# A graph-attention layer: in the steps of the softmax chain, look products ahead of kept-back products

## The chip, the cores and the metric

The kernel runs on one core of one Trainium2 chip. Its engines are TensorE (PE in the profile, with its weight loads as PEld), VectorE (DVE), ScalarE (ACT), GpSimd (POOL) and SyncE (SP). The metric is the device time of one execution in microseconds, median of three runs.

## The reference

12500 nodes with 64 features, 400000 edges with 64 features. Edges are sorted by destination, sources are random. Cut to what matters:

```
h_src = x[src]; h_dst = x[dst]
e     = leaky_relu(concat(h_src, h_dst, ef) @ W_attn + b_attn, 0.01)
m     = concat(h_src, ef) @ W_ne
emax  = segment_max(e, dst);  ex = exp(e - emax[dst])
alpha = ex / segment_sum(ex, dst)[dst]
z     = segment_sum(alpha * m, dst)
out   = relu(concat(x, z) @ W_out)
result = layernorm(x + out)
```

## The kernel before, in words

The edges are cut into groups of 512 (128 partitions times T = 4). Destinations are uneven: many edges go to the first nodes. Most groups go through 41 chunks of up to 16 groups, and a chunk through 4 lots of 4 groups. A chunk's course:

- **Gather.** For each group and t, POOL issues one indirect DMA (L331) that fetches 128 rows of a table by the edges' sources: 64 rows per chunk, numbered 0 to 63. POOL works a chunk ahead. The function `gather` ties certain rows to the step markers of the chunk in front (L53, below): row 28 is held until the last TensorE instruction that step 0 of the softmax had, row 33 until step 1's, 42 and 48 until step 2's and step 3's, 56 and 61 until the chunk's first and second products.
- **Scores.** VectorE and ScalarE work out the edge scores of each lot (L371 to L392).
- **Softmax.** A chain over the whole chunk (`softmax`, from L695 to L757): VectorE scans, two small matmuls to turn a column into a line (L599), a scan of the tops on one partition (L707, L708), a copy on ScalarE (L606, `line`), two small matmuls back into a column (L602), VectorE again from L717, L722 and L737 on ScalarE, and the same passage by L599, L741/L742, L606 and L602 for the denominators, then from L750 to L757 the weights. The chain has four breaks, in which TensorE would otherwise wait: `drawn` runs `dense_step(n)` there for n = 0 to 3.
- **Products.** `some_products` multiplies weighted one-hot destinations with gathered rows (L804, L809), two groups at a time, into a PSUM bank; VectorE adds the banks up (L828). Of a chunk's four lots two are multiplied right after the softmax; the other two are kept back ("later") and done in the softmax steps of the next chunk: four groups in step 0, two each in steps 1 and 2.

A second class of groups, 128 "dense" ones, is worked off beside the chunks. For each there is a *look* and a *count*. A look needs a one-hot row: `look_row` (L421) loads a row of 128 KB into the one buffer `low_of`, `look_turn` (L431, L432, ScalarE) makes the one-hot tile `big` from it, `look_products` (L442) makes four matmuls with it, each with a weight load and each shown as two instructions, into a bank of the ring `pg` (4 banks), and `look_scores` (L469 to L475, VectorE) picks the scores from them. A count (`dense_counts`) makes four tiles on ScalarE (L483, L484) and lows on VectorE (L486) and multiplies them (L491). Chunks 0 to 31 have looks: 128 in all, five in most of the first 18 chunks with looks, three or four in the others. The first of a chunk is made ahead of the softmax, the others in its steps: 96 of them, in 32 chunks.

The order of each engine is written by hand: what is called first in the program stands first in each engine's queue. So the order of calls in `dense_work(n)` is the order in which TensorE, ScalarE, VectorE and SP see that step's work. `seen` holds looks whose products were made, `turns` the one-hot tiles, `rows_ahead` the loaded rows. `latest()` returns the last TensorE instruction issued so far; behind each step it becomes the step's marker.

```
BEHIND = ((28, 0), (33, 1), (42, 2), (48, 3), (56, "first"), (61, "second"))
```

Of the kernel before, what the change touches and what calls it, by code (L numbers as in the profile page):

```python
# [59 lines left out]
def sorted_path(ctx, tc, x, dst, idx, edge, w_ne, w_attn, b_attn, w_out, out, flag):  # L60
# [52 lines left out]
    def nodes_of(g):  # L113
        return next(n for upto, n in NODS if g < upto)
# [303 lines left out]
    def look_row(g):  # L418

        row = work.tile([P, P * T], BF16, name="low_of", bufs=1)  # L420
        nc.sync.dma_start(out=row, in_=low_rows[g:g + 1].rearrange("g p t -> g (p t)").to_broadcast([P, P * T]))  # L421
        return row

    def big():
        return work.tile([P, P, T], F32, name="big", bufs=BIG)

    def look_turn(row):

        hot = big()
        flat_ = hot.rearrange("l p t -> l (p t)")  # L430
        nc.scalar.activation(flat_, row, AF.Square, bias=p_col)  # L431
        nc.scalar.activation(flat_, flat_, AF.Relu, scale=-1.0, bias=1.0)  # L432
        return hot

    def spare():
        return psum.tile([P, SG, P], F32, name="pg", bufs=4).rearrange("p a b -> p (a b)")

    def look_products(hot, bank_):

        found = bank_[:, 0:T * NB].rearrange("p (t h) -> p t h", t=T)  # L440
        for t in range(T):
            nc.tensor.matmul(found[:, t, :], hot[:, :, t], s_src, start=True, stop=True)  # L442
        return found
# [21 lines left out]
    def look_scores(g, found):  # L465

        pr = feats.tile([P, SG, T, D], F32, name="pr", bufs=1)
        hits = pr.rearrange("p g t f -> p (g t f)")[:, 0:T * NB].rearrange("p (t h) -> p t h", t=T)
        nc.vector.tensor_tensor(hits, count_[:, 0:NB].unsqueeze(1).to_broadcast([P, T, NB]),  # L469
                                high[:, :, g:g + 1].to_broadcast([P, T, NB]), op=OP.is_equal)  # L470
        nc.vector.tensor_tensor(hits, hits, found, op=OP.mult)  # L471
        picked = tiny.tile([P, T], F32, name="picked", bufs=1)
        nc.vector.tensor_reduce(picked, hits, axis=AX.X, op=OP.add)
        y = y_dense[:, :, kept_at(g)]
        nc.vector.tensor_tensor(y, y, picked, op=OP.add)  # L475
# [26 lines left out]
    def dense_sum(g, to):  # L502

        _, vs = nc.values_load_multi_w_load_instructions(
            rel[0:1, g:g + 1], engines=(EngineType.DVE,), min_val=0, max_val=ND - nodes_of(g),
            skip_runtime_bounds_check_because=within)
        n = min(FIT, nodes_of(g))
        at = counts[:, :, ds(vs[0], n)]
        nc.vector.tensor_tensor(at, at, to.rearrange("p (h n) -> p h n", n=n), op=OP.add)
        for j in range(nodes_of(g) - FIT):  # L510
            at = counts[:, :, ds(vs[0] + FIT + j, 1)]
            nc.vector.tensor_tensor(at, at, more_nodes[j].unsqueeze(2), op=OP.add)
# [77 lines left out]
    def node_sum(g0, z):  # L590

        at = accd[0:D, ds(node_of(g0), ND)]
        nc.vector.tensor_tensor(at, at, z, op=OP.add)
# [283 lines left out]
    with before:  # L877
# [23 lines left out]
        with tc.manual_schedule(engines={EngineType.DVE, EngineType.Pool, EngineType.Activation, EngineType.PE, EngineType.SP}):  # L901
# [30 lines left out]
            for g0 in range(0, NG, 3 * P):  # L932
                n = min(3 * P, NG - g0)
# [46 lines left out]
    def late_of(k):  # L980

        nc.vector.tensor_scalar(lates[:, k:k + 1], d0b[:, starts[k] + sizes[k] - 1:starts[k] + sizes[k]],
                                float(S - RING - zeroed[-1] * P), None, op0=OP.add)

    def raised():

        worst = tiny.tile([P, 4], F32, name="worst")
        bad = tiny.tile([P, 4], F32, name="bad")
        for i, (col, op) in enumerate(((fars, OP.max), (ups, OP.max), (lates, OP.max), (earlies, OP.min))):
            nc.vector.tensor_reduce(worst[:, i:i + 1], col, axis=AX.X, op=op)  # L990
        nc.vector.tensor_scalar(bad[:, 0:3], worst[:, 0:3], 0.0, None, op0=OP.is_gt)
        nc.vector.tensor_scalar(bad[:, 3:4], worst[:, 3:4], 0.0, None, op0=OP.is_lt)
        pbad = psum.tile([P, SG, P], F32, name="pg", bufs=4)[0:1, 0, 0:4]
        nc.tensor.matmul(pbad, ones_col, bad, start=True, stop=True)
        some = tiny.tile([1, 1], F32, name="some")
        nc.vector.tensor_reduce(some, pbad, axis=AX.X, op=OP.max)
        nc.vector.tensor_scalar(some, some, 1.0, None, op0=OP.min)
        nc.vector.tensor_copy(flag, some)
# [114 lines left out]
    with loop:  # L1113
# [9 lines left out]
        def add_up(most=SG * BG):  # L1123

            while sums and most:
                g0, n, pg, b0, fac = sums.pop(0)
                add_in(g0, n, pg, b0, fac)
                most -= 1
                k = starts.index(b0)
                if g0 + n == b0 + sizes[k]:  # L1130
                    done.extend(due[k])
# [3 lines left out]
        def some_products():  # L1135

            if later:
                k, g0, n, zx, w, b0, fac, g, pg = later[0]
                pg = bank(k) if pg is None else pg
                upto = min(n, g + SG // 2)  # L1140
                products(k, pg, zx, w, range(g, upto), n=n if g == 0 else None)
                later[0][7:] = [upto, pg]
                if upto == n:
                    later.pop(0)
                    behind.append((g0, n, pg, b0, fac))

        looks, counting, open_counts = list(range(DG)), [], []
        seen, dense_carry, resolved_at, at_rest = [], None, None, []
# [3 lines left out]
        def alike(todo, ends_=chunk_ends):  # L1152
            n = 0
            while n < min(each_of(todo[0]) if todo else 0, len(todo)) and not (n and todo[n] in edges_) and not (n and todo[n] in ends_):
                n += 1
            return [todo.pop(0) for _ in range(n)]
# [12 lines left out]
        with tc.manual_schedule(engines={EngineType.PE, EngineType.DVE, EngineType.Activation, EngineType.SP, EngineType.Pool}):  # L1169
            ready, turns = {}, []  # L1170
            resting, batch_looks, batch_counts = None, [], []
# [12 lines left out]
            for k, G in enumerate(sizes):  # L1184
# [7 lines left out]
                if k:  # L1192
                    joined = resting
                    batch_looks = alike(looks, ())
# [16 lines left out]
                for i, (g0, n) in enumerate(lots[k]):  # L1211
# [5 lines left out]
                    if k and i == 0 and batch_looks:  # L1217
                        loads = look_loads(batch_looks[0], len(batch_looks))
                        rows_ahead = [look_row(batch_looks[0])]
# [84 lines left out]
                def dense_step(n):  # L1304

                    nonlocal opened, summed, resolved_at, node_z
                    dense_work(n)
                    steps[n] = latest()

                def dense_work(n):  # L1310

                    nonlocal opened, summed, resolved_at, node_z
                    if n == 1 and final:
                        late_of(k)
                        raised()
                    if n == 0 and node_z:
                        node_sum(*node_z)
                        if node_z[0] + chunk_sizes[-1] == DG:
                            resolved_at = k
                        opened = node_z = None  # L1320
                    if seen:
                        look_scores(*seen.pop(0))
                    if n > 1 and behind:
                        sums.append(behind.pop(0))
                    add_up(1)
                    if n in (0, 2, 3):
                        while open_counts:
                            dense_sum(*open_counts.pop(0))
                    for half in range(2 if n == 0 else 1):
                        if later:  # L1330
                            some_products()
                    if n + 1 < len(batch_looks):
                        if n:
                            turns.append(look_turn(rows_ahead.pop(0)))
                            if n + 2 < len(batch_looks):
                                rows_ahead.append(look_row(batch_looks[n + 2]))
                        seen.append((batch_looks[n + 1], look_products(turns.pop(0), spare())))
                    inner = batch_counts[len(early_counts):]
                    for g in inner[n - 4:][:1] if len(inner) >= 4 - n > 0 else ():
                        open_counts.append(dense_counts(g))  # L1340
# [511 lines left out]
```

## Time and profile before

| what | us |
| --- | --- |
| median of 3 runs | 4620.77 |
| lowest and highest run | 4603.75, 4627.97 |
| the profiled execution | 4592.69 |
| its span | 4591.0 |
| PE busy | 2467.7 (54%) |
| POOL busy | 2480.1 (54%) |
| DVE busy | 2171.1 (47%) |
| ACT busy | 1364.4 (30%) |
| L442, matmuls, 1024 of them | 280.4 |
| L471, VectorE reading look products: busy, idle before it | 72.0, 511.2 |

The mean granted clock of TensorE was 0.653 in the profiled execution. In a row of the timeline the first number is the start in us from the span's start, the second the time in us; then come engine, line, operation, output and input, and how many instructions the row stands for. The brackets give the idle time of the engine before it and what ended it ("remote" is a signal whose sender the profile does not resolve to an instruction). In a row of the waits the numbers are us in total, times, and the longest in us.

### The profile page before, as it was taken

What the parts mean: (1) busy time and instruction counts of PE and PEld (TensorE: products, weight loads), DVE (VectorE), ACT (ScalarE), POOL (GpSimd) and SP (SyncE); (2) the same over time, 40 slices, a digit from 0 to 9 for tenths busy, and PEclk for the clock granted to TensorE, in tenths of its full rate; (3) what the DMA queues carried; (4) which work ended last, traced back from release to release, by engine and by line L of the source; (5) the groups of instructions that cost most, each with busy time, mean ns of one, the idle gap of its engine ahead of it and who ended that gap; (6) DMA issues with size and microseconds to landing.
All of it is one profiled execution on the core that took longest, in us unless ns stands there. A gap on an engine that the chain in (4) does not pass through costs nothing. (4 is left out here: it accounts for less than half of the span.)

```text
span 4591.0 us, 39135 instructions
## 1 busy us (share of the span) xinstructions
PE 2467.7 (54%) x10315; PEld 2017.7 (44%) x10315; DVE 2171.1 (47%) x5618; ACT 1364.4 (30%) x2963; POOL 2480.1 (54%) x2644
## 2 busy tenths in 40 slices
PE   0135455565566666666556555455455555555554
PEld 0135445454454445454444444334344444444454
DVE  4444444454445545455444454443444444444355
ACT  0111123243323323343333332232333333333212
POOL 7566655565554554645464646555454545565542
PEclk9999985555556556666666655556566656666655
DMA  8222322232222222222132222222221212222211
GB/s 111 64 56 60 76 61 60 58 78 58 58 62 62 62 55 50 64 48 64 39 69 44 60 59 54 52 54 45 45 59 43 61 37 54 49 51 50 43 37 35
DMA packets 452952, 257.79 MB, mean 56 GB/s; under 512 B 266314, under 2 KB 410801, under 8 KB 452722
## 3 DMA queue, kind: packets, MB, share of 16 engines
q1 hardware_dynamic: 367036, 167.23, 14.6%
q0 software_dynamic: 83936, 87.27, 11.6%
q8 instruction: 87, 1.43, 0.1%
q14 instruction: 143, 1.17, 0.1%
q10 hardware_dynamic: 1750, 0.70, 0.1%
HBM read 248.17 MB, written 6.80 MB: 56 GB/s over the span
## 5 line engine op out<-in xcount | busy, mean ns | idle before, releaser
L331 POOL DMA_INDIRECT zx<-table,srcs x2552 | 2409.8, 944 | 2026.9 <-issue 813.8
L809 PE MATMUL pg<-w,zx 128*128 128x16 f32 (+9 forms) x5088 | 1055.4, 376 | 174.0 <-issue 124.2
L809 PEld LDWEIGHTS pg<-w,zx 128*128 128x128 f32 x5088 | 1040.8, 312 | 189.4 <-issue 127.7
L491 PE MATMUL pg<-big,lows 128*128 128x490 f32 (+3 forms) x1024 | 608.6, 751 | 731.8 <-DVE lows L486 266.1
L491 PEld LDWEIGHTS pg<-big,lows 128*128 128x128 f32 x1024 | 278.9, 292 | 996.4 <-issue 598.0
L483 ACT ACTIVATE big<-places,place 128x490 f32<-128x490 int16 (+3 forms) x512 | 317.9, 621 | 597.4 <-remote 323.9
L376 DVE TENSOR_REDUCE fixed<-pr 128x16 f32<-128x1024 f32 (+2 forms) x168 | 201.5, 1199 | 302.9 <-ACT fixed L371 206.4
L442 PE MATMUL pg<-s_src,big 128*128 128x98 f32 x1024 | 280.4, 440 | 81.1 <-issue 80.5
L599 PE MATMUL lines<-ident,bnd 128*1 128x128 f32 x168 | 48.2, 387 | 499.7 <-ACT bnd L702 291.8
L471 DVE TENSOR_TENSOR pr<-pr,pg 128x392 f32<-128x392 f32 x128 | 72.0, 562 | 511.2 <-PE pg L442 312.4
L442 PEld LDWEIGHTS pg<-s_src,big 128*128 128x128 f32 x1024 | 255.3, 328 | 81.7 <-issue 81.3
L484 ACT ACTIVATE big<-big 128x490 f32<-128x490 f32 (+3 forms) x512 | 277.3, 542 | 16.3
L828 DVE TENSOR_TENSOR acc<-acc,pg 128x16 f32 (+9 forms) x654 | 121.7, 186 | 315.7 <-remote 205.9
L568 PE MATMUL pg<-xall,counts 128*128 128x256 f32 (+1 forms) x650 | 193.6, 447 | 121.1 <-issue 120.8
L599 PEld LDWEIGHTS lines<-ident,bnd 128*1 128x1 f32 x168 | 12.4, 96 | 521.0 <-ACT bnd L702 307.7
L371 ACT ACTIVATE fixed<-wrow 128x144 f32<-128x144 f32 (+8 forms) x168 | 44.3, 263 | 660.2 <-issue 188.9
L486 DVE TENSOR_SCALAR lows<-fixed,low,kept 128x128 f32<-128x128 f32 x512 | 175.7, 404 | 125.1 <-remote 103.3
L568 PEld LDWEIGHTS pg<-xall,counts 128*128 128x128 f32 (+1 forms) x650 | 146.2, 228 | 159.8 <-issue 137.5
L374 DVE TENSOR_TENSOR pr<-ze,lines 128x1024 f32<-128x1024 f32 (+2 forms) x168 | 198.7, 1183 | 5.0 <-DMA ze<-in_edge_dram 4.9
L552 PE MATMUL pg<-wd,ep 128*128 128x10 f32 (+5 forms) x512 | 107.9, 325 | 141.8 <-issue 141.7
L372 ACT ACTIVATE zx<-ze 128x1024 f32<-128x1024 f32 (+2 forms) x168 | 174.0, 1036 | 5.9 <-DMA zx<-table,srcs 1.0
L552 PEld LDWEIGHTS pg<-wd,ep 128*128 128x128 f32 x512 | 111.8, 306 | 143.5 <-issue 143.5
(308 smaller groups left out, 2715.3 us busy)
## 6 DMA issues: line engine op xcount, KB each, us to landing
ze<-in_edge_dram SPq DMA_DIRECT2D x157, 512.0 KB
zx<-table,srcs POOLq DMA_INDIRECT x2552
low_of<-low_rows SPq DMA_DIRECT2D x128, 128.0 KB
ep<-in_edge_dram SPq DMA_DIRECT2D x128, 128.0 KB
wrow<-wins SPq DMA_DIRECT2D x152, 96.0 KB
ed<-in_edge_dram SPq DMA_DIRECT2D x14, 640.0 KB
ed<-in_edge_dram SPq DMA_DIRECT2D x14, 384.0 KB
table<-xall SPq DMA_DIRECT2D x7, 455.0 KB
```

Source lines behind the costliest of these rows:

```text
L331: row = nc.gpsimd.indirect_dma_start(out=zx[0:r, g, t, 1:EW] if plain else zx[0:r, g, t, 0:EW], out_offset=None, in_=x[:, :] if plain else ...
L372: nc.scalar.activation(zx[0:r, 0:n, :, EW:EW + D], ze[0:r, 0:n], AF.Copy)
L374: nc.vector.tensor_tensor(pr[0:r, 0:n], ze[0:r, 0:n], w_edge[0:r].unsqueeze(1).to_broadcast([r, n, T, D]), op=OP.mult)
L376: nc.vector.tensor_reduce(ysum[0:r, 0:n], pr[0:r, 0:n], axis=AX.X, op=OP.add)
L442: nc.tensor.matmul(found[:, t, :], hot[:, :, t], s_src, start=True, stop=True)
L483: nc.scalar.activation(hi, places[:, 0:wide], AF.Square, bias=place[:, t, g:g + 1])
L484: nc.scalar.activation(hi, hi, AF.Relu, scale=-1.0, bias=1.0)
L486: nc.vector.tensor_scalar(lows[t], count_, low[:, t, g:g + 1], kept[:, t, kept_at(g):kept_at(g) + 1], op0=OP.is_equal, op1=OP.mult)
L491: nc.tensor.matmul(to, lows[t], highs[t], start=(t == 0), stop=(t == T - 1))
L552: nc.tensor.matmul(z[:, h:h + 2], rows_, cols, start=(i == 0), stop=(i + 1 == len(steps)), skip_group_check=True).ins
L568: nc.tensor.matmul(pairs[0:m * ND, 0:m * D], counts[:, h0:h0 + m, :].rearrange("l h n -> l (h n)"), xall[:, h0:h0 + m, 1:EW], start=(h0 == ...
L809: nc.tensor.matmul(pg[:, g, :], zx[:, g, t, 1:EW + D], w[:, g, t, :], start=(t == 0), stop=(t == T - 1)).ins
```

## The change

In `dense_work(n)` the block for the next look is moved ahead of `some_products`, and within the block the products come ahead of the turn of the look after it. Its conditions move by one step too: the tile for look n + 2 is made in step n, where it was made in step n + 1, and the row for look n + 3 is asked for in step n.

```diff
                     if n in (0, 2, 3):
                         while open_counts:
                             dense_sum(*open_counts.pop(0))
+                    if n + 1 < len(batch_looks):
+                        seen.append((batch_looks[n + 1], look_products(turns.pop(0), spare())))
+                        if n + 2 < len(batch_looks):
+                            turns.append(look_turn(rows_ahead.pop(0)))
+                            if n + 3 < len(batch_looks):
+                                rows_ahead.append(look_row(batch_looks[n + 3]))
                     for half in range(2 if n == 0 else 1):
                         if later:
                             some_products()
-                    if n + 1 < len(batch_looks):
-                        if n:
-                            turns.append(look_turn(rows_ahead.pop(0)))
-                            if n + 2 < len(batch_looks):
-                                rows_ahead.append(look_row(batch_looks[n + 2]))
-                        seen.append((batch_looks[n + 1], look_products(turns.pop(0), spare())))
                     inner = batch_counts[len(early_counts):]
```

TensorE, the softmax steps of a chunk with five looks and two inner counts; a row of the order counts program instructions (the profile shows each of these matmuls twice). From L599 (the tops' line) to the second L602 (the denominators):

```order
 L599 MATMUL lines<-ident,bnd 1x4x32 x2
+L442 MATMUL pg<-s_src,big 128x98 x4
 L804 MATMUL pg<-zx,ident 1x4x8
 L809 MATMUL pg<-w,zx 128x20 x16
-L442 MATMUL pg<-s_src,big 128x98 x4
-L602 MATMUL lines<-ident,line 128x1 x2
+L602 MATMUL lines<-ident,line 128x1 x2
+L442 MATMUL pg<-s_src,big 128x98 x4
 L804 MATMUL pg<-zx,ident 1x4x8
 L809 MATMUL pg<-w,zx 128x20 x8
-L442 MATMUL pg<-s_src,big 128x98 x4
-L599 MATMUL lines<-ident,bnd 1x4x32 x2
+L599 MATMUL lines<-ident,bnd 1x4x32 x2
+L442 MATMUL pg<-s_src,big 128x98 x4
```

In each step the four look matmuls now stand directly behind the chain's own pair of matmuls (L599 or L602) and ahead of the kept-back products, which now end the step. Step 2 goes on in the same way: its L809 now stands behind its L442. The orders of VectorE, POOL and SP are the same in both kernels.

ScalarE, from the boundary of the first scan (L702) to that of the second (L737):

```order
 L702 ACTIVATE bnd<-soft 128x2
-L606 ACTIVATE line<-tops 1x256
-L431 ACTIVATE big<-low_of,p_col 128x512
-L432 ACTIVATE big<-big 128x512
-L722 ACTIVATE soft<-turned 128x128
-L732 ACTIVATE over<-over 1x1
-L733 ACTIVATE dens<-dens,over 1x1
-L737 ACTIVATE bnd<-soft 128x2
+L431 ACTIVATE big<-low_of,p_col 128x512
+L432 ACTIVATE big<-big 128x512
+L606 ACTIVATE line<-tops 1x256
```

A one-hot tile now stands ahead of the tops' line (L606), the next ahead of L722, and the last behind L737: each one step ahead of where it stood.

## The prediction

> **What bounds the kernel now.** I read the page's busy shares first, then the totals of the waits, then one chunk (the tenth, which starts its softmax at 1071.5 us) engine by engine in the timeline.
>
> ```profile
> span 4591.0 us, 39135 instructions
> PE 2467.7 (54%) x10315; PEld 2017.7 (44%) x10315; DVE 2171.1 (47%) x5618; ACT 1364.4 (30%) x2963; POOL 2480.1 (54%) x2644
> POOL zx L331 <- PE pg L442: 779.6, 34, 42.9
> DVE pr L471 <- PE pg L442: 312.4, 63, 12.5
> DVE acc L828 <- remote: 205.9, 26, 14.6
> ```
>
> No engine is busy much over half of the span, so the chunks are bound by a ring of waits. The third row says where POOL stands still: 34 times, 779.6 us in all, it waits with a gather for a look product (L442). The fourth is VectorE waiting for a look product, 312.4 us. That last figure is what the change aims at, and the question is how much of it lies on the ring.
>
> POOL's column in the tenth chunk shows the ring:
>
> ```profile
> 1083.82 0.94 POOL L331 DMA_INDIRECT zx<-table,srcs  x1 [22.73 <-PE pg L442]
> 1085.07 0.94 POOL L331 DMA_INDIRECT zx<-table,srcs  x1 [0.30 <-issue]
> 1090.05 0.94 POOL L331 DMA_INDIRECT zx<-table,srcs  x1 [0.30 <-PE lines L599]
> 1100.05 0.94 POOL L331 DMA_INDIRECT zx<-table,srcs  x1 [0.30 <-issue]
> 1104.13 0.94 POOL L331 DMA_INDIRECT zx<-table,srcs  x1 [3.14 <-PE pg L442]
> 1112.12 0.94 POOL L331 DMA_INDIRECT zx<-table,srcs  x1 [0.81 <-PE pg L491]
> 1120.87 0.95 POOL L331 DMA_INDIRECT zx<-table,srcs  x1 [0.30 <-issue]
> 1124.47 0.94 POOL L331 DMA_INDIRECT zx<-table,srcs  x1 [2.65 <-remote]
> ```
>
> A gather is asked for every 1.25 us (1085.07 - 1083.82). Row 28 of the next chunk's 64 waits for the last matmul of step 0 and comes at 1083.82; rows 28 to 41 then run without a stop until 1100.99; row 42 waits 3.14 us for step 2, row 48 0.81 us for step 3, row 56 2.65 us for the chunk's own products after the softmax. So the softmax steps can lengthen the ring in four places: the way from the chunk's first softmax instruction to row 28, and the waits before rows 42, 48 and 56, which together make 6.6 us of about 112 per chunk (4591.0 us over 41 chunks).
>
> TensorE and VectorE over the same steps:
>
> ```profile
> 1073.85 0.59 PE L599 MATMUL lines<-ident,bnd 128*1 128x128 f32 x2 [5.58 <-ACT bnd L702]
> 1074.56 7.01 PE L809 MATMUL pg<-w,zx 128*128 128x20 f32 x32
> 1081.41 2.14 PE L442 MATMUL pg<-s_src,big 128*128 128x98 f32 x8
> 1083.48 0.37 PE L602 MATMUL lines<-ident,line 1*128 1x1 f32 x2
> 1083.97 3.60 PE L809 MATMUL pg<-w,zx 128*128 128x20 f32 x16
> 1087.40 2.14 PE L442 MATMUL pg<-s_src,big 128*128 128x98 f32 x8
> 1089.33 0.64 PE L599 MATMUL lines<-ident,bnd 128*1 128x128 f32 x2
> 1089.76 3.44 PE L809 MATMUL pg<-w,zx 128*128 128x20 f32 x16
> 1093.03 2.14 PE L442 MATMUL pg<-s_src,big 128*128 128x98 f32 x8
> 1097.82 0.29 PE L602 MATMUL lines<-ident,line 1*128 1x1 f32 x2
> ```
>
> ```profile
> 1083.58 0.56 DVE L471 TENSOR_TENSOR pr<-pr,pg 128x392 f32<-128x392 f32 x1 [8.14 <-PE pg L442]
> 1084.86 0.36 DVE L717 SCALAR_TENSOR_TENSOR soft<-pen,lines,soft 128x128 f32<-128x128 f32 x1
> 1089.58 0.56 DVE L471 TENSOR_TENSOR pr<-pr,pg 128x392 f32<-128x392 f32 x1 [1.95 <-PE pg L442]
> 1091.33 0.81 DVE L828 TENSOR_TENSOR acc<-acc,pg 128x20 f32 x4 [0.39 <-issue]
> 1093.33 0.26 DVE L741 TENSOR_TENSOR_SCAN dens<-rw,lines 1x64 f32<-1x64 f32 x1
> 1103.73 0.56 DVE L471 TENSOR_TENSOR pr<-pr,pg 128x392 f32<-128x392 f32 x1 [9.44 <-PE pg L442]
> 1105.49 0.81 DVE L828 TENSOR_TENSOR acc<-acc,pg 128x20 f32 x4 [0.40 <-issue]
> 1108.33 0.34 DVE L750 SCALAR_TENSOR_TENSOR soft<-mask,lines,soft 128x128 f32<-128x128 f32 x1
> ```
>
> TensorE has no gap between 1073.85 and 1097.82. And one thing looks odd: the look product of step 2 ends at 1095.17 by its row, while VectorE, which waits for it, starts only at 1103.73. POOL's uninterrupted run ended at 1100.99, so the start is 2.74 us behind the end of that run, like row 42's (3.14 us). Inside the same run the product of step 1 (ended 1089.54, 5.7 us after the run's start) was seen at 1089.58. So in this trace a completion of TensorE reaches the others at once early in a run of gathers, and late in it only behind the run's end. Where between 5.7 and 11.4 us (1095.17 - 1083.82) the border lies, the rows do not say.
>
> The Trainium skill, page "Perfetto Trace Analysis", section "Tensor Engine Instruction (MATMUL, LD_WEIGHTS)", says that the end shown for a matmul is computed from its size and not observed; by it the product may really have ended late, rather than its signal. Every sum below uses only when the waiting engine starts, so it holds by both readings; by the page's, fewer matmuls ahead of a product would bring it forward even late in a run, which is the second case of step 2 below, always: 14 us instead of 7. No row here separates the two.
>
> **The change, step by step.** Nothing is added or taken away: 128 looks, the same matmuls, the same VectorE order. Of the 128, 96 stand inside softmax steps, in 32 chunks.
>
> Step 0. The look product moves ahead of the 32 kept-back matmuls, 7.01 us sooner. VectorE's four score instructions, now behind its 8.14 us wait, run under those matmuls. L717 then waits for L602 alone, which ends at 1083.85, instead of coming at 1084.86: 1.0 us sooner. Row 28 does not gain: it waits for the last matmul of the step, and 0.59 + 7.01 + 2.14 is the same sum in either order. First term: 0.
>
> Step 1. L717 to L737 (the boundary for the second scan) come 1.0 us sooner, but L599 stands on TensorE behind L602, the kept-back products and the look product: 0.37 + 3.60 + 2.14 us without a gap up to 1089.33, again in either order. The 1.0 us is absorbed: 0. The marker for row 33 also stands where it stood, at about 1089.5; it must come within 6.24 us of row 28 (1090.05 - 1083.82) for the run not to stop, and has 0.5 us to spare.
>
> Step 2. The scores of look 2 no longer wait 1.95 us, so L741 comes about 2 us sooner; L602 behind it stands on TensorE behind products and counts until 1097.82, so that is absorbed too. The product of look 3 moves ahead of 3.44 us of kept-back products: it ends at 1089.97 + 2.14 = 1092.1, 8.3 us into POOL's run, where it ended 11.4 us into it. If that is before the border, its scores (1103.73 to 1105.49, 1.76 us) are done inside the run, and L828, which now waits longest since its products end at 1095.5, starts at about 1103.7: L750 is 1.76 us sooner. If not, both signals come at the run's end and nothing changes.
>
> What that is worth on the ring: row 48 need not wait 0.81 us, so rows 48 to 55 end 0.8 us sooner, and row 56 (2.65 us behind their end) comes 0.8 us sooner. The rest of the 1.76 us is hidden by those eight gathers. Only chunks with four or five looks have such a product in step 2: 18 of them. With the border unknown between 5.7 and 11.4 us, and 8.3 about in the middle, I take half: 18 x 0.8 x 0.5 = 7 us. Ends: 0 and 14 us.
>
> ScalarE. Each one-hot row is made one step sooner, so in step 0 its two instructions stand ahead of the tops' line (L606):
>
> ```profile
> 1073.63 0.17 ACT L702 ACTIVATE bnd<-soft 128x2 f32<-128x2 f32 x1 [1.37 <-DVE soft L700]
> 1075.08 0.66 ACT L606 ACTIVATE line<-tops 1x256 f32<-1x256 f32 x1 [1.28 <-DVE tops L708]
> 1075.65 0.70 ACT L431 ACTIVATE big<-low_of,p_col 128x512 f32<-128x512 bf16 x1
> 1076.38 0.63 ACT L432 ACTIVATE big<-big 128x512 f32<-128x512 f32 x1
> 1076.38 12.02 SPq L421 DMA_DIRECT2D low_of<-low_rows  x2
> ```
>
> 1.33 us of work goes into a gap of 1.28 us, so L606 is at most some 0.1 us late, and L602 that reads it stands behind 7 us of matmuls: 0. Without that cover it would be 0.1 x 32 = 3 us. The row's DMA (L421, one buffer) is issued when the turn before it has read, now at about 1074.6 instead of 1076.4, with SP's order unchanged; the turn of step 1 needs it ahead of L722, at 1085.97, eleven us later. Cost 0; if the row came later than that, each us would delay L722 and L737.
>
> Sum: 0 + 0 - 7 + 0 = -7 us against the profiled execution's 4592.69 us, or 4586. That execution lies 0.6% below the median of the runs shown, 4620.77; in the median's measure it is 4613 us.
>
> **Rivals.** *Faster, through row 56.* If look 3's scores pass in nearly all 18 chunks, L750 comes 1.76 us sooner, and the first products with it, so that their completion may reach POOL before its run of eight gathers is long enough to hide it; then the 2.65 us before row 56 go too. That is 0.81 + 2.65 = 3.5 us in 18 chunks, 62 us; with half of the row-56 waits gone, 18 x (0.81 + 1.3) = 38 us, 4583. For it speaks that several waits here are the price of signals that miss a run by little; against it, that row 56 is asked for at 1122.1 and the products would end around 1120.3, still late in that run. A naive account, that VectorE's 312.4 us of waiting is all saved, is refuted by TensorE's gapless rows.
>
> *Slower, through row 33.* In the thirteenth chunk POOL did stop there:
>
> ```profile
> 1428.44 0.94 POOL L331 DMA_INDIRECT zx<-table,srcs  x1 [35.08 <-PE pg L442]
> 1438.97 0.94 POOL L331 DMA_INDIRECT zx<-table,srcs  x1 [4.59 <-PE lines L599]
> 1460.51 0.94 POOL L331 DMA_INDIRECT zx<-table,srcs  x1 [3.14 <-remote]
> ```
>
> Row 48 came 32.07 us behind row 28 there, against 28.30 in the tenth (1112.12 - 1083.82): 3.8 us more. The marker of step 1 is now the last kept-back product and not a look product; if it comes over 0.5 us later than now, because step 1's look product waits for its bank or its one-hot row, or because the products behind it load weights more slowly, a chunk falls into this pattern. 27 of the 32 chunks could; a third of them makes 9 x 3.8 = 34 us, 4655. Against it: the sum of the step's matmuls is the same, and its one-hot row was ready by 1077.
>
> *Nothing at all.* Every signal behind the border stays behind it, and the gain is 0: 4621, inside the forecast's band.
>
> **Chances.** Half a per cent, 23 us, is about what a measurement of this kernel tells from no change. Forecast together with nothing at all: 0.51. Faster through row 56 or a like threshold: 0.34. Slower through row 33 or a like stop: 0.15. The likeliest case by itself reaches from 4600 to 4630, the spread of the runs shown around 0 to 14 us. The range takes in most of the faster rival (38 us, and half way from it to 62 us) and the nearer part of the slower: 4565 to 4645.
>
> **What would show it.** Right in step 0: L471's first wait falls from 8 us to about 1, L717 stands directly behind L602, and the distance from L695 to row 28 stays 12.3 us (1083.82 - 1071.52):
>
> ```profile
> 1071.52 0.32 DVE L695 STREAM_TRANSPOSE turned<-soft 128x128 f32<-128x128 f32 x1
> ```
>
> Right in step 2: POOL still runs 14 gathers from row 28 in most chunks, and L828 takes over the wait of L471 that ended 2.7 us behind the run, so that the waits for look products shrink in the totals while those of L828 grow by a like amount. Wrong on the fast side: row 56 follows row 55 without a wait. Wrong on the slow side: runs of five gathers from row 28 in chunks that had fourteen. Wrong altogether: the distance from L695 to row 28 changes, or a chunk's stretch behind L757, which I left as it is, does.

## The result, and the profile after

| | before | after |
| --- | --- | --- |
| median, 18 runs each | 4620.39 us | 4587.9 us |
| lowest and highest | 4582.47, 4659.99 | 4550.85, 4622.36 |
| the profiled execution's span | 4591.0 us | 4611.6 us |

The ratio is 0.9933, 95% interval 0.991 to 0.9957: 0.67% faster, by 0.43 to 0.90%. The forecast was 4613 us, and 4565 to 4645 as the range. The executions of one kernel lie 1.7% apart, and the profiled one of the changed kernel is slower than the profiled one of the kernel before. The one stands at the slow end of its kernel's runs, the other at the quick end. So the traces below show how the mechanism has changed; how much it is worth is taken from the timed runs alone.

The page of the changed kernel and the totals of its waits (us in total, times, longest):

```profile
span 4611.6 us, 39038 instructions
POOL zx L331 <- PE pg L809: 854.3, 36, 42.1
DVE counts L509 <- remote: 246.5, 29, 18.3
DVE acc L828 <- remote: 238.6, 32, 14.8
DVE soft L717 <- PE lines L602: 196.7, 37, 6.2
DVE pr L471 <- PE pg L442: 12.3, 21, 0.8
```

Two of these rows as they were in the kernel before:

```profile
DVE counts L509 <- remote: 101.4, 17, 14.7
DVE soft L717 <- PE lines L602: 38.8, 9, 6.0
```

VectorE's wait for look products fell from 312.4 us to 12.3 us. It went where the prediction put it, to L717, which now waits for L602 (38.8 to 196.7 us), and in part to L828 (205.9 to 238.6 us); and also to L509, which adds up a count's products (101.4 to 246.5 us). POOL waits about as long for the end of step 0 (779.6 and 103.9 us for L442 and L809 before, 854.3 us for L809 now), only the name of the matmul has changed. VectorE's idle time as a whole, the span less what it is busy, is 2419.9 us before and 2433.7 us now: in these two executions the change has moved waiting and removed none.

The tenth chunk again, which starts its softmax at 1055.08 us in this execution. POOL (start, duration, wait in brackets):

```profile
1067.21 0.94 POOL L331 DMA_INDIRECT zx<-table,srcs  x1 [21.98 <-PE pg L809]
1074.60 0.94 POOL L331 DMA_INDIRECT zx<-table,srcs  x1 [1.45 <-PE lines L599]
1092.07 0.94 POOL L331 DMA_INDIRECT zx<-table,srcs  x1 [0.30 <-issue]
1096.37 0.94 POOL L331 DMA_INDIRECT zx<-table,srcs  x1 [3.35 <-remote]
```

TensorE in step 1, with the kept-back products now ending it at 1073.07 us, 5.86 us after row 28:

```profile
1066.87 0.37 PE L602 MATMUL lines<-ident,line 1*128 1x1 f32 x2
1067.16 2.19 PE L442 MATMUL pg<-s_src,big 128*128 128x98 f32 x8
1069.47 3.60 PE L809 MATMUL pg<-w,zx 128*128 128x20 f32 x16
1072.91 0.59 PE L599 MATMUL lines<-ident,bnd 128*1 128x128 f32 x2
```

VectorE:

```profile
1055.08 0.32 DVE L695 STREAM_TRANSPOSE turned<-soft 128x128 f32<-128x128 f32 x1
1059.84 0.56 DVE L471 TENSOR_TENSOR pr<-pr,pg 128x392 f32<-128x392 f32 x1 [0.83 <-PE pg L442]
1067.34 0.36 DVE L717 SCALAR_TENSOR_TENSOR soft<-pen,lines,soft 128x128 f32<-128x128 f32 x1 [6.14 <-PE lines L602]
1074.40 0.28 DVE L741 TENSOR_TENSOR_SCAN dens<-rw,lines 1x64 f32<-1x64 f32 x1 [0.35 <-PE lines L599]
1075.48 0.56 DVE L471 TENSOR_TENSOR pr<-pr,pg 128x392 f32<-128x392 f32 x1
1086.89 0.36 DVE L750 SCALAR_TENSOR_TENSOR soft<-mask,lines,soft 128x128 f32<-128x128 f32 x1 [1.83 <-issue]
```

Read against the rows of before: row 28 comes 12.13 us after L695 (1067.21 - 1055.08), where it came 12.30 us after it. The difference is that POOL now stops at row 33: five gathers, then a stop of 1.45 us (the row names L599, which stands directly behind the step's marker), and then fifteen without a stop (1074.60 to 1093.01). The scores of look 3 start at 1075.48, 0.9 us into the new run and without a wait, where they waited 9.44 us for the end of a run of fourteen. L750 comes 31.8 us after L695, where it came 36.8 us after it (1108.33 - 1071.52). But POOL pays for the stop: row 48 comes 29.2 us after row 28 (1096.37 - 1067.21), where it came 28.3.

So two accounts were possible. **Theory A:** the stop at row 33 is the gain, since it opens POOL's run and TensorE's completions get through. **Theory B:** the gain is that VectorE's part of each step comes 1 to 2 us sooner, and the stop costs. Every experiment is compared with the kernel before on the same chip.

### The profile page after: what moved, and what is told of

Its sections match the earlier page's. It is cut to its first block, busy times and chain, and to the rows that moved or that the text cites. A ratio compares the mean times of both kernels' runs of the same rounds, so it can differ in the third digit from the quotient of the medians.

```text
span 4611.6 us, 39038 instructions
## 1 busy us (share of the span) xinstructions
PE 2480.4 (54%) x10315; PEld 2023.9 (44%) x10315; DVE 2177.9 (47%) x5618; ACT 1370.0 (30%) x2963; POOL 2478.8 (54%) x2644
## 3 DMA queue, kind: packets, MB, share of 16 engines
q0 software_dynamic: 83936, 87.27, 11.4%
## 5 line engine op out<-in xcount | busy, mean ns | idle before, releaser
L331 POOL DMA_INDIRECT zx<-table,srcs x2552 | 2408.9, 944 | 2049.4 <-PE pg L809 854.3
L809 PE MATMUL pg<-w,zx 128*128 128x16 f32 (+9 forms) x5088 | 1060.1, 376 | 250.2 <-issue 195.7
L809 PEld LDWEIGHTS pg<-w,zx 128*128 128x128 f32 x5088 | 1045.3, 313 | 261.9 <-issue 194.1
L491 PE MATMUL pg<-big,lows 128*128 128x490 f32 (+3 forms) x1024 | 628.5, 771 | 665.0 <-DVE lows L486 233.9
L491 PEld LDWEIGHTS pg<-big,lows 128*128 128x128 f32 x1024 | 282.3, 296 | 943.5 <-issue 718.6
L483 ACT ACTIVATE big<-places,place 128x490 f32<-128x490 int16 (+3 forms) x512 | 318.6, 622 | 581.4 <-remote 278.6
L599 PE MATMUL lines<-ident,bnd 128*1 128x128 f32 x168 | 47.4, 382 | 519.5 <-ACT bnd L702 308.8
L442 PE MATMUL pg<-s_src,big 128*128 128x98 f32 x1024 | 272.0, 434 | 72.9 <-issue 72.9
L828 DVE TENSOR_TENSOR acc<-acc,pg 128x16 f32 (+9 forms) x654 | 121.7, 186 | 365.5 <-remote 238.6
L442 PEld LDWEIGHTS pg<-s_src,big 128*128 128x128 f32 x1024 | 253.4, 328 | 83.5 <-issue 79.1
L599 PEld LDWEIGHTS lines<-ident,bnd 128*1 128x1 f32 x168 | 10.8, 96 | 541.9 <-ACT bnd L702 326.1
L509 DVE TENSOR_TENSOR counts<-counts,pg 128x490 f32 (+3 forms) x128 | 75.0, 586 | 357.3 <-remote 246.5
L552 PE MATMUL pg<-wd,ep 128*128 128x10 f32 (+5 forms) x512 | 108.8, 329 | 113.2 <-issue 110.4
L552 PEld LDWEIGHTS pg<-wd,ep 128*128 128x128 f32 x512 | 111.3, 308 | 111.1 <-issue 111.0
```

The source lines that it names most:

```text
L331: row = nc.gpsimd.indirect_dma_start(out=zx[0:r, g, t, 1:EW] if plain else zx[0:r, g, t, 0:EW], out_offset=None, in_=x[:, :] if plain else ...
L483: nc.scalar.activation(hi, places[:, 0:wide], AF.Square, bias=place[:, t, g:g + 1])
L491: nc.tensor.matmul(to, lows[t], highs[t], start=(t == 0), stop=(t == T - 1))
L552: nc.tensor.matmul(z[:, h:h + 2], rows_, cols, start=(i == 0), stop=(i + 1 == len(steps)), skip_group_check=True).ins
L809: nc.tensor.matmul(pg[:, g, :], zx[:, g, t, 1:EW + D], w[:, g, t, :], start=(t == 0), stop=(t == T - 1)).ins
```

## The experiments on the stop

**Without the tie of row 33.** The changed kernel, POOL having no reason to stop in step 1:

```diff
-BEHIND = ((28, 0), (33, 1), (42, 2), (48, 3), (56, "first"), (61, "second"))
+BEHIND = ((28, 0), (42, 2), (48, 3), (56, "first"), (61, "second"))
```

> The changed kernel, with the tie of row 33 to step 1's marker taken out, so that POOL has no reason to stop between rows 28 and 41. In the changed kernel's profile POOL stopped at row 33 (five gathers, then 1.45 us) in most chunks that had run through 14 gathers before. Theory A (the stop is the gain: it lets TensorE's signals of steps 2 and 3 through, which were held until 2.7 us behind a run of 14): runs of 14 from row 28 are back, and so is the time, ratio to the kernel before 0.997 to 1.003. Theory B (the gain is the 1.0 to 2 us by which VectorE's steps come sooner, and the stop costs): the ratio stays at 0.993 or falls to 0.987, 18 stops of 1.45 us being 26 us.

Measured: 0.9997 [0.9968, 1.0025], 4619.95 us. The gain is gone, though the order of the steps is that of the changed kernel. Its tenth chunk, POOL and VectorE:

```profile
1091.42 0.94 POOL L331 DMA_INDIRECT zx<-table,srcs  x1 [22.38 <-PE pg L809]
1111.84 0.94 POOL L331 DMA_INDIRECT zx<-table,srcs  x1 [3.21 <-remote]
```

```profile
1091.56 0.36 DVE L717 SCALAR_TENSOR_TENSOR soft<-pen,lines,soft 128x128 f32<-128x128 f32 x1 [6.14 <-PE lines L602]
1109.19 0.56 DVE L471 TENSOR_TENSOR pr<-pr,pg 128x392 f32<-128x392 f32 x1 [9.59 <-remote]
```

POOL runs fourteen gathers, and look 3's scores wait 9.59 us again, although its product ended 8.1 us into the run and not 11.4. L717 has its 1.0 us and it buys nothing. For the gain, theory B falls.

**The stop alone.** The kernel before, its order of the steps untouched, with step 1's marker tied to row 32, which POOL asks for 5.0 us after row 28:

```diff
-BEHIND = ((28, 0), (33, 1), (42, 2), (48, 3), (56, "first"), (61, "second"))
+BEHIND = ((28, 0), (32, 1), (42, 2), (48, 3), (56, "first"), (61, "second"))
```

> The kernel before, with step 1's marker tied to row 32 and not to row 33. Row 32 is asked for 5.0 us behind row 28, ahead of the look product's end at 5.7 us, so POOL stops for about 0.8 us in step 1 and the order of TensorE is untouched. Theory A: the stop alone brings the gain, ratio 0.991 to 0.996, and L471's wait of 9.4 us in step 2 is gone. Theory B: 1.000 to 1.004, as POOL loses 0.8 us in up to 27 chunks.

Measured: 0.9962 [0.9935, 0.9988], 4597.05 us. Theory A's side: a stop by itself makes the kernel before faster, by 0.38%, a little above half of the change's gain by the middle values; the intervals overlap. In its tenth chunk L471's wait in step 2 is 2.42 us:

```profile
1084.90 0.95 POOL L331 DMA_INDIRECT zx<-table,srcs  x1 [1.77 <-ACT big L483]
```

```profile
1091.33 0.56 DVE L471 TENSOR_TENSOR pr<-pr,pg 128x392 f32<-128x392 f32 x1 [2.42 <-PE pg L491]
```

The stop was 1.77 us and not the 0.8 us expected: the marker's product ended 5.7 us after row 28, and POOL went on at 6.5 us (1084.90 - 1078.43, row 28 of this execution below). What held it for the last 0.7 us is not known; the row names ScalarE's L483.

```profile
1078.43 0.95 POOL L331 DMA_INDIRECT zx<-table,srcs  x1 [30.95 <-PE pg L442]
```

**The change, with the stop one row earlier.** The same edit in the changed kernel.

> The changed kernel with step 1's marker tied to row 32: POOL has stopped by 4.7 us behind row 28, before the last kept-back product ends at 5.9 us, so that product's signal should come at once and not 1.2 us behind the run's end. The stop then ends at about 6.1 us and not at 7.4 us, and rows 33 on come 1.3 us sooner in some 18 chunks. Theory A: ratio to the kernel before 0.987 to 0.992 (23 us less than the change). Theory B: the same direction and size. The run tells only whether the length of the stop matters: if it doesn't, 0.993.

Measured: 0.9933 [0.9902, 0.9965], 4578.99 us: the same as the change. The expected further 23 us did not come. In its tenth chunk the stop ends 6.6 us after row 28 (1074.78 - 1068.17) instead of 7.4, so only 0.8 of the 1.3 us could be had per chunk, and the interval of 0.3% does not show that.

```profile
1068.17 0.95 POOL L331 DMA_INDIRECT zx<-table,srcs  x1 [20.48 <-PE pg L809]
1074.78 0.95 POOL L331 DMA_INDIRECT zx<-table,srcs  x1 [1.91 <-ACT big L483]
```

**Step 1 as before.** The changed kernel, with the look product behind the kept-back products in step 1 alone:

```diff
+                    moved = n != 1
+                    if not moved:
+                        for half in range(2 if n == 0 else 1):
+                            if later:
+                                some_products()
                     if n + 1 < len(batch_looks):
                         seen.append((batch_looks[n + 1], look_products(turns.pop(0), spare())))
 ...
-                    for half in range(2 if n == 0 else 1):
-                        if later:
-                            some_products()
+                    if moved:
+                        for half in range(2 if n == 0 else 1):
+                            if later:
+                                some_products()
```

> The changed kernel with step 1 as before on TensorE: its look product stands behind the kept-back products again, steps 0 and 2 keep the change, and every one-hot row is made one step sooner as in the change. Step 1's marker is then a look product as before. Theory A: no stop at row 33, runs of 14, ratio 0.997 to 1.003. Theory B: L717 and the scores of steps 0 and 2 keep most of what they gained, 0.993 to 0.996.

Measured: 1.0046 [1.0024, 1.0068], 4634.09 us. No gain, as theory A has it, but also slower than its band, by an amount clear of noise. In the tenth chunk L741 comes 9.38 us after L717, where it came 8.47 us after it (1093.33 - 1084.86), so the 1.0 us that step 0 won is lost again in step 1, where the scores still wait for a look product behind the kept-back ones:

```profile
1081.99 0.36 DVE L717 SCALAR_TENSOR_TENSOR soft<-pen,lines,soft 128x128 f32<-128x128 f32 x1 [6.14 <-PE lines L602]
1091.37 0.26 DVE L741 TENSOR_TENSOR_SCAN dens<-rw,lines 1x64 f32<-1x64 f32 x1
```

That accounts for no gain, not for 0.46% of loss. A low clock does not account for it either: four of the twelve runs had a granted clock of 0.608 to 0.621, but the other eight (0.641 to 0.649) have a median of 4633.5 us. The loss stays open.

**The one-hot rows alone**, the order of the products as before (`moved = False` in the edit above):

> The changed kernel with the look products behind the kept-back products in all steps, as before; only the one-hot rows are made one step sooner. Theory A (the stop at row 33 is the gain): no stop, ratio to the kernel before 0.998 to 1.002. Rival C (the sooner one-hot rows carry a part of the gain): 0.994 to 0.997. Rival D (they cost, which would explain the 0.46% by which the variant with step 1 as before was slower): 1.003 to 1.006.

Measured: 0.9986 [0.9951, 1.0021], 4592.01 us against 4594.4. No difference is measured. Rival D (1.003 to 1.006) lies outside the interval and falls, also as the cause of the loss above. Rival C (0.994 to 0.997) is not needed, but the interval reaches into its band.

**Step 1 alone** (`moved = n == 1`):

> The changed kernel with the look product ahead of the kept-back products in step 1 alone; steps 0, 2 and 3 as before, one-hot rows one step sooner. Step 1's marker is then a kept-back product. Theory A: the stop at row 33 is there, ratio 0.991 to 0.996, about the whole gain. Theory B (VectorE's sooner steps): the scores of step 0 stand behind the kept-back products again, L717 is late by 1 us again, ratio 0.998 to 1.002.

Measured: 1.0024 [0.999, 1.0058], 4598.46 us. As a forecast of theory A this missed: 0.991 to 0.996 was expected. Its POOL rows tell why. The tenth and the eleventh chunk:

```profile
1088.15 0.94 POOL L331 DMA_INDIRECT zx<-table,srcs  x1 [22.57 <-PE pg L442]
1094.41 0.94 POOL L331 DMA_INDIRECT zx<-table,srcs  x1 [0.30 <-issue]
...
1195.71 0.94 POOL L331 DMA_INDIRECT zx<-table,srcs  x1 [21.11 <-PE pg L442]
1203.05 0.94 POOL L331 DMA_INDIRECT zx<-table,srcs  x1 [1.39 <-PE lines L599]
```

In one chunk POOL passes row 33 without a stop, in the next it stops. The last kept-back product of step 1 ends 5.86 us after row 28 in both. In the kernel before, the marker ends at the latest 5.72 us after row 28 in the chunks without an inner count in that step, and never makes POOL stop there. With the new order of step 1 it ends 5.86 to 5.90 us after row 28 in 23 chunks, and POOL stops in some and not in others: in 16 of the 23 in the changed kernel, in 2 of the 23 here. So the stop that the expectation took for certain comes only in some chunks, and the time of the marker alone does not settle it. Whether the order of steps 0 and 2 makes the difference, or something else in these two executions, the traces do not tell.

Counted in POOL's timeline: the 36 chunks with a tie at row 28, by the gathers that run from there, and the 27 chunks from chunk 5 to chunk 31, by whether POOL runs 36 gathers without a stop from row 56 on or stops before row 61 and runs 31:

| kernel | stop at row 32 or 33 | run of 36 | run of 31 | ratio |
| --- | --- | --- | --- | --- |
| before | 5 | 11 | 16 | 1 |
| changed | 21 | 7 | 20 | 0.9933 |
| changed, no tie of row 33 | 0 | 11 | 16 | 0.9997 |
| before, tie at row 32 | 30 | 9 | 18 | 0.9962 |
| changed, tie at row 32 | 30 | 4 | 23 | 0.9933 |
| changed, step 1 as before | 5 | 11 | 16 | 1.0046 |
| one-hot rows alone | 5 | 11 | 16 | 0.9986 |
| step 1 alone | 7 | 8 | 19 | 1.0024 |

The counts are of one execution each, the ratios of many. The three kernels with many stops are the three that are faster. The second pair of columns suggests where the sooner L750 pays. Up to row 56 POOL is not ahead of the kernel before (row 56 comes 42.3 us after row 28 on average over the 27 chunks, where it came 41.7). But chunks with the run of 36 last 119.2 us on average from L695 to L695 in the kernel before, and those with the run of 31 last 111.0 us. The changed kernel has four fewer of the long kind: 4 x 8.2 = 33 us, and the medians differ by 32.5 us. That agrees, but the two executions that were counted do not show this gain (4613.35 us for the changed kernel, 4592.69 us for the kernel before), there is one count each, and the step-1-alone kernel is against it (three fewer of the long kind, no gain). So it is an account and not a proof. What a long run costs was therefore tested by itself.

## The experiments on long runs

In the kernel before, the stretch behind the tenth chunk's softmax. POOL's run of 36 begins at 1124.47 and ends at 1169.09; ScalarE, VectorE and TensorE:

```profile
1168.15 0.94 POOL L331 DMA_INDIRECT zx<-table,srcs  x1 [0.30 <-issue]
...
1175.11 0.54 ACT L483 ACTIVATE big<-places,place 128x294 f32<-128x294 int16 x1 [40.29 <-remote]
...
1175.15 0.73 DVE L486 TENSOR_SCALAR lows<-fixed,low,kept 128x128 f32<-128x128 f32 x2 [30.10 <-remote]
...
1140.02 0.41 PE L491 MATMUL pg<-big,lows 128*128 128x294 f32 x1 [1.55 <-issue]
1176.18 4.29 PE L491 MATMUL pg<-big,lows 128*128 128x294 f32 x8 [35.75 <-ACT big L484]
...
1187.59 0.32 DVE L695 STREAM_TRANSPOSE turned<-soft 128x128 f32<-128x128 f32 x1
```

ScalarE's last instruction ends at 1134.82, TensorE's last product at 1140.43 and VectorE's last at 1145.05; all three then stand still until 1175, some six us behind the end of POOL's run, though the next chunk's own gathers were done eight rows into that run. If the run is what holds them, breaking it must pay far more than the stop at row 33.

**Four breaks in the changed kernel.** Gathers 3, 9, 15 and 21 of each chunk wait for the landing of the gather just ahead:

```diff
+BREAKS = (3, 9, 15, 21)
 ...
+                if (g0 + g - b0) * T + t in BREAKS and last_row and not plain:
+                    tc.add_manual_dep(row.ins, last_row[0].name,
+                                      mybir.DependencyInfo(mybir.DependencyClass.Sync, mybir.DependencyReason.DATA),
+                                      reason="a run of gathers is broken here")
+                last_row[:] = [row.ins]
```

> The changed kernel, with gathers 3, 9, 15 and 21 of each chunk waiting for the landing of the gather just ahead of them, so that the run of 31 or 36 gathers is broken into pieces of six. Theory A as a rule for all runs: in the long run ScalarE and VectorE stand still for some 30 us per chunk (L483 40.3 us before chunk 11's softmax in the kernel before) because TensorE's signals are held; broken up, the next chunk's scores and softmax start sooner, the wait before row 28 (779.6 us in all) shrinks, ratio 0.90 to 0.97 even though POOL loses 4 x 1 to 2 us per chunk. If the hold in the long run is something else (data that really comes late), POOL's loss shows: 41 x 4 x 1.5 = 246 us less what the 20 to 40 us in front of row 28 hide, ratio 1.00 to 1.03.

Measured: 0.8708 [0.8661, 0.8754], 3992.97 us. Its page and waits, and the tenth chunk from L695 to the next (L703 here; lines behind the edit are shifted, L483 is L491):

```profile
span 3992.3 us, 39163 instructions
POOL zx L334 <- DMA zx<-table,srcs: 339.7, 193, 4.1
ACT big L491 <- remote: 197.4, 31, 19.6
...
1052.88 0.94 POOL L334 DMA_INDIRECT zx<-table,srcs  x1 [3.10 <-DMA zx<-table,srcs]
1062.24 0.94 POOL L334 DMA_INDIRECT zx<-table,srcs  x1 [2.18 <-DMA zx<-table,srcs]
...
1047.58 0.54 ACT L491 ACTIVATE big<-places,place 128x294 f32<-128x294 int16 x1 [1.71 <-PE pg L450]
...
969.38 0.32 DVE L703 STREAM_TRANSPOSE turned<-soft 128x128 f32<-128x128 f32 x1
1065.44 0.32 DVE L703 STREAM_TRANSPOSE turned<-soft 128x128 f32<-128x128 f32 x1
```

The breaks cost POOL 339.7 us and the kernel is some 600 us faster, more than the 0.90 to 0.97 that was expected. The chunk lasts 96.1 us instead of 116.1, ScalarE's longest wait for TensorE in this stretch is below two us where it was 40.29, and the wait before row 28, 779.6 us in all before, is no longer among the large ones: POOL now sets the pace.

**The same breaks in the kernel before:**

> The kernel before, with gathers 3, 9, 15 and 21 of each chunk waiting for the landing of the gather just ahead of them; the order of the steps is the one before. If the change is worth only what its extra stops are worth (theory A), it should be worth less once the long runs are broken anyway: ratio to the kernel before 0.868 to 0.874, the same as the changed kernel with the same breaks (0.871). If the order of the steps has a worth of its own where signals come through: 0.874 to 0.885, the changed kernel with breaks being better.

Measured: 0.8687 [0.865, 0.8724], 3996.51 us. That is level with the changed kernel with the same breaks, each against the kernel before on its own chip: with the long runs broken the change is worth nothing that can be measured. This fits theory A, by which its gain was the opening of runs. It is no proof of it, since where POOL sets the pace a gain of VectorE's would be hidden too.

**Nine breaks, behind the last gather and behind the one before it:**

```diff
-BREAKS = (3, 9, 15, 21)
+BREAKS = (3, 9, 15, 21, 27, 33, 38, 45, 51)
```

> The changed kernel with nine such breaks per chunk (gathers 3, 9, 15, 21, 27, 33, 38, 45 and 51), so that no run in the softmax steps is over six gathers either. If the hold is by the length of the run: the softmax chain's holds (L750 waited 12.9 us on average with four breaks, 21 gathers running from row 21) shrink to 5 us or less and the waits in front of rows 42 and 56 go, against five more stops of about 2 us; ratio 0.83 to 0.87. If the stops cost more than the holds that they end: 0.87 to 0.90.

> The same nine breaks, but each waits for the landing of the gather two ahead of it, so that a stop is about 1.25 us shorter (0.5 to 1 us and not 2). If any stop lets the held signals through: better than nine breaks behind the last gather by up to 41 x 9 x 1.25 = 460 us less what POOL did not need, ratio 0.78 to 0.84. If a stop has to last over some microseconds to let them through: the holds of the long runs are back in part, 0.87 to 0.95.

Measured: 0.8959 [0.8911, 0.9007] and 0.9369 [0.9303, 0.9434]. The waits of the first, then of the second:

```profile
POOL zx L334 <- DMA zx<-table,srcs: 794.2, 368, 6.9
POOL zx L334 <- PE pg L817: 15.1, 8, 2.7
```

```profile
POOL zx L334 <- DMA zx<-table,srcs: 232.2, 274, 4.5
POOL zx L334 <- PE pg L817: 529.2, 26, 39.9
ACT big L491 <- remote: 284.7, 44, 41.6
```

Nine full stops free the others (POOL hardly waits for TensorE any more, 15.1 us for the kept-back products), but POOL pays 794.2 us and sets the pace. The nine shorter stops cost POOL only 232.2 us, and the holds are back: ScalarE waits up to 41.6 us and POOL 529.2 us in front of row 28. So it seems that a stop has to last: with 0.8 us on average (232.2/274) little gets through, with 2.2 us (794.2/368) nearly all. But the two versions also differ in how often POOL really stops, 274 and 368 times, and the runs do not part the two.

**Three and two breaks in the kernel before** (gathers 3, 10, 17; gathers 4 and 16):

> The kernel before with three breaks (gathers 3, 10 and 17), runs of seven gathers (8.7 us) and one stop fewer than with four, about 2 us per chunk or 82 us in all where POOL sets the pace. If seven in a row still let signals through in time: ratio 0.85 to 0.868. If the border that the steps showed (5.9 us) holds everywhere, the holds grow by more than the stop saved: 0.872 to 0.90.

> The kernel before with two breaks (gathers 4 and 16), runs of twelve (15 us). Two stops fewer than with four, 164 us in all where POOL sets the pace; but the next chunk's scores wait for signals through runs of 15 us. If the holds decide: 0.89 to 0.94. If two openings per chunk suffice: 0.84 to 0.868.

Measured: 0.8738 [0.8677, 0.8798] and 0.9093 [0.9026, 0.916]. Three are level with four within the interval, which just reaches both cases of the expectation; with two the holds decide. Between too few and too many, four breaks (or three) lie at the bottom, and no version that was run is faster than these, some 600 us below both kernels.

## Why the prediction came out as it did

The number was within the range, and the direction of the likeliest case's term (7 us faster) was right; the size, 32.5 us, lies in the faster rival's band of 0.34 and not in the band of 0.51. It got there by a way that no case had, through a stop that the prediction priced as a loss. So that the time fell within the range is luck.

- *What was read rightly.* That TensorE's sums in steps 0 and 1 do not change, that row 28 would not gain, that L717 would gain 1.0 us and lose it again behind TensorE: as measured (12.13 us against 12.30 us to row 28; no gain without the tie of row 33).
- *Step 1, the term that failed.* "The marker for row 33 also stands where it stood, at about 1089.5", and the run "has 0.5 us to spare". The marker moved by 0.14 us only, from 5.72 to 5.86 us after row 28, still ahead of 6.24 us. But the step counted the spare time from the end of the matmul, as if its signal came at once. The trace records when TensorE's semaphore moved for it: 7.13 us after row 28, behind the end of POOL's five gathers. In the changed kernel with the tie at row 32, where POOL had already stopped, a marker that ends at the same 5.86 us is signalled 0.02 us later, and so it is in all the 23 chunks. So the run of gathers held the signal, and POOL stopped.
- *The border.* "With the border unknown between 5.7 and 11.4 us": the runs show a signal passing at 5.72 us, and held or passed at 5.86 to 5.90 us. Half a gain for look 3 at 8.3 us inside a run of 14 was too much; without the stop its scores waited 9.59 us. With the stop they start 0.9 us into a new run. The mechanism (a product that ends late in a run is seen only behind it) was right, its term for step 2 rested on the wrong side of the border.
- *The slower rival.* It named the stop at row 33, and the runs of five gathers came (in 21 chunks, where there were 5). But its condition, a marker over 0.5 us later, was not met, and its price had the wrong sign. It took 3.8 us from a chunk whose marker really ends 10 us after row 28; the stop here is 1.45 us, and it opens a run that had held up everything behind it.
- *The faster rival.* The gain was to come at row 56; row 56 is not sooner (41.0 us after row 28 now, by 1108.22 - 1067.21; 40.65 before). By the counts it came before row 61, in the long run.
- *ScalarE.* Cost nothing, as said: the kernel with the one-hot rows alone is level with the kernel before. Its one new wait is harmless, too: L431 in step 0 waited 2.64 us for the row (L421) that is asked for 1.9 us earlier, 2.9 us after L695 where it was 4.9, in a gap of over seven us.

```profile
1061.89 0.72 ACT L431 ACTIVATE big<-low_of,p_col 128x512 f32<-128x512 bf16 x1 [2.64 <-DMA low_of<-low_rows]
1108.22 0.94 POOL L331 DMA_INDIRECT zx<-table,srcs  x1 [2.18 <-remote]
```

What the prediction missed as a whole: it read the hold behind a run of gathers as a fixed cost of some 3 us, and did not look at the same hold in the longest run, where the engines stood still for 30 us and more.

## What to carry to other kernels

When an engine's start lies a constant few us behind the end of another engine's uninterrupted run, rather than behind its own producer, ask what that run costs everywhere, the longest run first, before moving work inside a step. A stop that looks like a loss can be the opening that others wait for: here four stops of about 2 us per chunk made 13%, and the reordering made 0.7% only as far as it happened to cause a stop. And a margin that is counted from the modelled end of a matmul is none where the signal of that matmul can be held: here 0.5 us to spare was not enough.

## What the runs showed of the hardware that was not expected

While GpSimd issues indirect gathers back to back, one per 1.25 us, the progress of TensorE's work reaches other engines promptly only for the first six us or so of the run (passed at 5.72 us in all chunks, stopped or passed at 5.86 to 5.90 us), and then often only behind the run's end. Breaking the runs by stops of about 2 us each lets it through; with stops of 0.8 us the holds are back in part.

The trace shows that finished work is signalled late, and not only that TensorE falls behind its modelled ends. It records the times at which TensorE's semaphore moved. In the tenth chunk of the kernel before, seven instructions that move it end between 1095.17 and 1102.69 by their rows. It moved for them at 1103.70, 1103.75, 1103.79, 1103.83, 1103.87, 1103.92 and 1104.01, 0.04 to 0.09 us apart, while the four of them that belong to a count (L491) start 0.49 to 0.97 us apart by their rows. Work that was still being done would end at its own pace, not in such a burst. TensorE does fall behind a little too: the last of these matmuls start at 1100.10 and 1102.20, after 0.65 and 1.86 us in which TensorE waited for nothing that the profile shows. In the run of 36, a product (L552) that ends at 1133.90 is signalled at 1174.32. That trace has 39 bursts of three or more signals from TensorE, each at most 0.06 us behind the last, and none begins inside a run of gathers. ScalarE's semaphore has no such burst, VectorE's has one. Where on its way a signal is held, these runs do not tell. Nor do they say why step 1's marker, as a kept-back product, is let through in some chunks and not in others at the same 5.86 us.
